# Reading already transposed tokens from DRAM in place of transposing them on TensorE, in a gated cross-attention block

## The chip, the cores and the metric

The kernel runs on one core of one Trainium2 chip. The metric is the device time of one execution in microseconds (us). Each kernel is timed in several runs and the median is given; one further execution is recorded by the hardware profiler, and every duration below is from that one.

TensorE is called PE in the profile (PEld is its weight load), VectorE DVE, ScalarE ACT, GpSimd POOL and SyncE SP. DMAs are issued from SP's queue, but for a few at the start that ACT issues.

## What is computed

The input is x, two sequences of 2048 tokens of 512 numbers (4096 tokens in all), and a context of two times 77 tokens.

```python
def layernorm(x):  # no learned scale
    return (x - mean(x)) / sqrt(var(x) + 1e-5)

x = x + tanh(g_xattn) * xattn(layernorm(x), ctx, ctx)   # 16 heads of 32, softmax over 77 keys
x = x + tanh(g_ffn) * ffn(layernorm(x))                 # 512 -> 2048 -> gelu -> 512

def qlinear(x, w, b):          # both linears of ffn
    xq, sx = quant(x)          # round(x / scale), scale = max|x| / 127 over the whole tensor
    wq, sw = quant(w)
    return (xq @ wq.T + b) * (sw * sx)
```

All arrays are float32. The maximum in the quantization is over a whole tensor, so the first linear of the feed-forward can't start before the attention of every token is done.

## The kernel before

The tokens are worked in eight blocks of 512 (`NB` = 8, `TB` = 512), numbered 0 to 7 here; each block is four tiles of 128 tokens (`NT` = 4). There are three stages: attention over blocks 0 to 7, then the first linear with gelu, then the second linear. Blocks 0 to 3 belong to the first sequence, 4 to 7 to the second.

Attention of block i goes through eight steps s = 0 to 7 (loop at lines 473 to 532). A step treats one group of four heads (g = s // 2) and half of the block's tokens (two tiles):

- `apply_v` (line 343), in even steps: softmax weights times values, for the group before. Result `pc` in PSUM, copied to `cT` by ACT.
- `softmax` (line 294), two steps ahead of the step that uses it: PE computes the scores `ps`; DVE takes the maximum (line 312) and subtracts it (316), ACT takes the exponential (322), DVE sums (324) and takes the reciprocal (326), POOL multiplies (327).
- `transpose_a` (line 333), twice: PE transposes the softmax weights (`pta`), ACT copies them to `aT`.
- `project_o` (line 358) in even steps, for the block before: output projection `po`; DVE adds it to X with the gate (line 369).
- `project_q` (line 281) in odd steps: query projection of four matmuls, each of which the profile records as two. At s = 1 and 3 it works on block i, at s = 5 and 7 on block i + 1.
- Only for the next block: `norm(i + 1)` at s = 1 (mean and variance of four tiles by two DVE instructions each, lines 159 and 160; then 1/sigma on POOL, line 163), and `transpose_x(i + 1, t)`, tiles 0 and 1 at the end of s = 3, tiles 2 and 3 at the start of s = 5. `transpose_x` (line 265) has DVE write (x - mean)/sigma (270), PE transpose it in four pieces (275, `ptx`) and ACT copy it to `xnT` (276), which `project_q` reads.
- At s = 7, for the block before: `norm2_stats` and `norm2_max` (lines 371 and 375): mean, variance and 1/sigma of the new X, then its normalized form `xf` (line 189) and the maximum of that, `tm` (line 384).
- In blocks 1 to 4 `weight_step` (line 406) has DVE prepare the feed-forward weights in odd steps: at i = 1 and 3 the maximum of a quarter of w1 or w2 (line 405), at i = 2 and 4 its quantization (lines 204 and 205). After the last maximum `diagonal_of` (line 166) makes a diagonal matrix (`diag_w`, line 171), and at s = 0 of the next block `scale_of` (line 174) puts a matmul on PE (`pg_w`, line 178) that waits for it.
- `add_bias` (line 278) on POOL.

The order on PE is the program's own (`manual_schedule` for PE). The orders on DVE, ACT and POOL are set when the kernel is built, by a list scheduler that follows the program with some freedom; `issue_after` forbids it to put an instruction ahead of a given one. Once built, each engine takes its instructions strictly in that order, and SP its DMAs too.

X blocks and the raw quarters of w1 and w2 share a pool of eight buffers of 1 MB (`xpool`), so a weight quarter is loaded when another tile has been used up. `load_x(i + 2)` stands after block i. PSUM results of `project_q`, `project_o`, `apply_v` and `scale_of` share two buffers (`ps_p`); those of the transposes share two others (`ps_t`), scores two more (`ps_s`).

Of the kernel before, what the change touches and what calls it, by code (L numbers as in the profile page):

```python
# [8 lines left out]
F32 = mybir.dt.float32  # L9
# [6 lines left out]
P = 128  # L16
D = 512
# [25 lines left out]
def tile_flamingo_gated_block(  # L43
    ctx: ExitStack,
    tc: tile.TileContext,
    x: bass.AP,
    ctxT: bass.AP,
    g_xattn: bass.AP,
# [37 lines left out]
    def kchunks(w):  # L86
        return w.rearrange("(kc p) n -> p kc n", p=P)
# [6 lines left out]
    wo_sb = awts.tile([P, KC, D], F32, name="wo_sb")  # L94
    ctx_sb = awts.tile([P, B, KC, NK], F32, name="ctx_sb")
    kblk = [awts.tile([P, NG, RK], F32, name=f"kb{b}") for b in range(B)]
    vblk = [awts.tile([NK, D], F32, name=f"vb{b}") for b in range(B)]
    work = actx.enter_context(tc.tile_pool(name="work", bufs=2))
    bv_sb = work.tile([NK, D], F32, tag="cT", name="bv_sb", bufs=7)
    bq_sb = const.tile([P, KC], F32, name="bq_sb")  # L100
    bk_sb = const.tile([P, KC], F32, name="bk_sb")
# [10 lines left out]
    def load_ctx(engine, b):  # L112
        engine.dma_start(ctx_sb[:, b, :, :], kchunks(ctxT[b]))

# [14 lines left out]
    for b in range(1, B):  # L129
        load_ctx(nc.sync, b)  # L130
    load_x(1)
    nc.sync.dma_start(wo_sb, kchunks(woT))
    nc.sync.dma_start(tg[:, 0:1], g_xattn.to_broadcast([P, 1]))
    nc.sync.dma_start(tg[:, 1:2], g_ffn.to_broadcast([P, 1]))
    nc.sync.dma_start(bo_sb, bo.to_broadcast([P, D]))
    nc.sync.dma_start(b1_sb, b1)

    ident = const.tile([P, P], F32, name="ident")
# [72 lines left out]
    with actx:  # L211
# [7 lines left out]
        def project_k(b, g):  # L219

            pk = ps_p.tile([P, 512], F32, tag="pp", name=f"pk{b}_{g}")
            for kc in range(KC):
                nc.tensor.matmul(  # L223
                    pk[:, :NK],
                    wk_sb[:, kc, g * P : (g + 1) * P],
                    ctx_sb[:, b, kc, :],
                    start=(kc == 0),
                    stop=(kc == KC - 1),
                )
            return pk  # L230
# [12 lines left out]
        def project_v(b):  # L243

            pv = ps_p.tile([P, 512], F32, tag="pp", name=f"pvv{b}")
            for kc in range(KC):
                nc.tensor.matmul(  # L247
                    pv[:NK, :],
                    ctx_sb[:, b, kc, :],
                    wv_sb[:, kc, :],  # L250
                    start=(kc == 0),
                    stop=(kc == KC - 1),
                )
            nc.vector.tensor_tensor(vblk[b], pv[:NK, :], bv_sb, ALU.add)

        ln, xnT, qT, aT, cT, es = {}, {}, {}, {}, {}, {}

        def norm(i):
# [4 lines left out]
            ln[i] = mv, rstd  # L263

        def transpose_x(i, t):
            mv, rstd = ln[i]
            if t == 0:
                xnT[i] = work.tile([P, KC, TB], F32, tag="xnT", name=f"xnT{i}", bufs=1)
            xn = work.tile([P, D], F32, tag="xn", name=f"xn{i}_{t}")
# [11 lines left out]
        def project_q(i, g):  # L281
            pq = ps_p.tile([P, TB], F32, tag="pp", name=f"pq{i}_{g}")
            for kc in range(KC):
                nc.tensor.matmul(  # L284
                    pq,
                    wq_sb[:, kc, g * P : (g + 1) * P],
                    xnT[i][:, kc, :],
                    start=(kc == 0),
                    stop=(kc == KC - 1),
                )  # L290
            qT[i, g] = work.tile([P, TB], F32, tag="qT", name=f"qT{i}_{g}", bufs=5)
            nc.scalar.activation(qT[i, g], pq, AF.Identity, bias=bq_sb[:, g : g + 1])  # L292
# [126 lines left out]
        def weight_step(i, s):  # L419
# [53 lines left out]
        for i in range(NB):  # L473
            for s in range(2 * NG):
# [42 lines left out]
                with tc.issue_after(last["DVE"]):  # L517
                    weight_step(i, s)
                    if i == NB - 1 and s == 5:

                        xs0 = work.tile([P, NT, D], F32, tag="aT", name="xs0", bufs=3)
                        for t in range(NT):
                            normalize2(xs0[:, t, :], 0, t)
                t = s - NT if i == 0 else s // 2
                if t >= 0 and (i == 0 or s % 2 == 0):
                    with tc.issue_after(last["POOL"]):
                        add_bias(i, t)
            if i + 2 < NB:
                load_x(i + 2)
            if i == 0:  # L530
# [15 lines left out]
        s_x, inv_x = scale_of(diagonal_of(xmax, "x"), "x", ps_p, "pp")  # L546
        xq0 = work.tile([P, NT, D], BF16, tag="xnT", name="xq0", bufs=1)
        for t in range(NT):
# [218 lines left out]
```

## Time and profile before

| what | value |
|---|---|
| median of 3 runs | 656.1 us (653.93 to 656.38) |
| the profiled execution's own time | 654.98 us |
| its span, first to last instruction | 653.2 us |
| what lies around the span | 1.8 us |
| mean granted PE clock | 0.986 |
| busy: PE, DVE, ACT, POOL | 625.5, 520.1, 337.3, 205.1 us |
| attention stage, 57 to 411 us: PE busy | 347.1 of 354.0 us |
| attention stage: DVE, ACT, POOL busy | 293.5, 150.3, 125.4 us |
| DMA in the attention stage | 43 GB/s, 12% of the 16 engines |

The stages follow each other: attention to about 411 us, the first linear to about 530 us, the second to the end. A busy time is a union of intervals and not a sum; consecutive DVE instructions overlap by some 0.08 us in the records, so the distance from start to start is the better price of one instruction, and it is used below.

### The profile page before, as it was taken

How to read it: one execution, taken by the hardware profiler on the slowest of the kernel's cores; microseconds unless marked ns; L12 is line 12 of the kernel's file. 1: busy time of each engine (PE TensorE's matmuls, PEld its weight loads, DVE VectorE, ACT ScalarE, POOL GpSimd, SP SyncE). 2: the span in 40 equal slices, each digit the busy share in tenths (PEclk: the TensorE clock that was granted, in tenths of full speed). 3: DMA queues.
4: the chain of work that ended last, by engine and by line, in shares of the span. 5: the costliest groups of instructions: out<-in, count | busy, mean ns of one | idle time of the engine just before them, and what ended most of it. 6: DMA issues, size and time to landing. Idle time of an engine off the chain costs nothing.

```text
span 653.2 us, 8220 instructions
## 1 busy us (share of the span) xinstructions
PE 625.5 (96%) x3048; PEld 318.2 (49%) x3048; DVE 520.1 (80%) x825; ACT 337.3 (52%) x463; POOL 205.1 (31%) x161
## 2 busy tenths in 40 slices
PE   5999999999999999999999999599999979999997
PEld 4565555555554554555555543244444434444443
DVE  5685787998998998976877768899989779877551
ACT  2365444444444354354343441298888879654530
POOL 2144333234243334233242331000000009997000
PEclk9999999999999999999999999599999999999999
DMA  9902000031131131100000000189999109799952
GB/s 281 374 35 99 31 1 1 2 129 64 65 129 69 62 129 64 66 1 0 1 1 1 2 18 0 21 285 306 334 342 331 25 0 368 251 348 347 343 196 80
DMA packets 44255, 84.90 MB, mean 130 GB/s; under 512 B 18795, under 2 KB 22891, under 8 KB 38584
## 3 DMA queue, kind: packets, MB, share of 16 engines
q1 hardware_dynamic: 43112, 83.70, 36.5%
q10 hardware_dynamic: 1104, 0.69, 0.3%
q8 instruction: 24, 0.39, 0.3%
q14 instruction: 15, 0.12, 0.1%
HBM read 49.25 MB, written 31.46 MB: 124 GB/s over the span
## 4 chain that ended last, share of the span: by engine, by line
PE 80%; DVE 15%; ACT 2%; POOL 1%; issue 1%; DMA 1%; ACTq 0%; DVEq 0%
PE pf L684 17%; PE ph L620 17%; PE po L362 14%; PE pq L284 12%; PE pta L340 7%; PE ps L303 5%; PE pc L349 3%; DVE xf L189 2%; DVE tm L384 2%; PE ptx L275 2%; DVE e L316 2%; DVE mx L312 2%; PE pvv L247 1%; DVE sm L324 1%; PE pk L223 1%; ACT e L322 1%
## 5 line engine op out<-in xcount | busy, mean ns | idle before, releaser
L327 POOL TENSOR_TENSOR e<-e,rs 128x616 f32<-128x616 f32 x64 | 78.7, 1229 | 223.1 <-DVE rs L326 148.9
L284 PE MATMUL pq<-xnT,wq_sb 128*128 128x512 f32 x256 | 115.3, 593 | 0.0
L684 PE MATMUL pf<-w2q,hq 128*128 128x512 bf16 x512 | 112.4, 383 | 2.6 <-DVE hq L205 2.0
L362 PE MATMUL po<-wo_sb,cT 128*128 128x512 f32 x256 | 114.8, 593 | 0.0
L620 PE MATMUL ph<-xqT,w1q 128*128 128x512 bf16 x512 | 113.1, 385 | 0.7 <-DVE xqT L560 0.7
L627 ACT ACTIVATE G<-ph,b1s,s 128x512 f32<-128x512 f32 x128 | 99.5, 777 | 15.1 <-PE ph L620 4.3
L341 ACT COPY aT<-pta 77x512 f32<-77x512 f32 x128 | 68.0, 581 | 68.9 <-PE pta L340 68.8
L322 ACT ACTIVATE e<-e 128x616 f32<-128x616 f32 x64 | 45.9, 717 | 87.9 <-DVE e L316 86.3
L637 DVE TENSOR_REDUCE hmax<-G 128x1 f32<-128x1024 f32 (+1 forms) x65 | 76.8, 1198 | 8.0 <-ACT G L627 7.9
L684 PEld LDWEIGHTS <-hq 128*128 128x128 bf16 x512 | 50.4, 99 | 64.3 <-issue 2.4
L620 PEld LDWEIGHTS <-w1q 128*128 128x128 bf16 x512 | 50.6, 99 | 62.9 <-issue 3.2
L340 PE MATMUL pta<-ident,e 128*77 128x128 f32 x512 | 70.2, 280 | 0.4 <-ACT xnT L276 0.4
L324 DVE TENSOR_REDUCE sm<-e 128x8 f32<-128x616 f32 x64 | 50.6, 790 | 24.4 <-ACT e L322 24.1
L362 PEld LDWEIGHTS po<-wo_sb,cT 128*128 128x128 f32 x256 | 46.4, 190 | 48.2 <-issue 46.6
L284 PEld LDWEIGHTS pq<-xnT,wq_sb 128*128 128x128 f32 x256 | 46.1, 190 | 46.1 <-issue 46.1
L677 ACT ACTIVATE Gb<-Gb,inv_h 128x2048 f32<-128x2048 f32 x22 | 43.7, 1999 | 35.7 <-DMA Gb<-h 35.7
L312 DVE TENSOR_REDUCE mx<-ps 128x8 f32<-128x616 f32 x64 | 50.2, 784 | 14.8 <-PE ps L303 14.3
L340 PEld LDWEIGHTS pta<-ident,e 128*77 128x77 f32 x512 | 55.6, 147 | 11.8 <-issue 10.3
L698 POOL TENSOR_TENSOR x<-x,b_sb 128x512 f32<-128x512 f32 x32 | 57.2, 1829 | 0.1
L303 PEld LDWEIGHTS ps<-kb,qT 64*128 64x128 f32 x512 | 36.0, 186 | 43.5 <-ACT qT L292 20.6
L316 DVE TENSOR_TENSOR e<-ps,mx 128x616 f32<-128x616 f32 x64 | 50.9, 796 | 2.5
L303 PE MATMUL ps<-kb,qT 64*128 64x154 f32 x512 | 50.6, 317 | 0.3 <-ACT qT L292 0.2
(89 smaller groups left out, 592.7 us busy)
## 6 DMA issues: line engine op xcount, KB each, us to landing
h<-G SPq DMA_DIRECT2D x22, 1024.0 KB, 5.6
Gb<-h SPq DMA_DIRECT2D x22, 1024.0 KB, 7.7
raw_w<-in_w2T SPq DMA_DIRECT2D x8, 1024.0 KB, 5.0
out_y<-x SPq DMA_DIRECT2D x32, 256.0 KB, 3.1
x<-in_x SPq DMA_DIRECT2D x7, 1024.0 KB, 5.2
raw_w<-in_w1T SPq DMA_DIRECT2D x4, 1024.0 KB, 11.7
wk_sb<-in_wkT SPq DMA_DIRECT2D x4, 256.0 KB, 5.4
wq_sb<-in_wqT SPq DMA_DIRECT2D x4, 256.0 KB, 6.3
```

The source lines that it names most:

```text
L284: nc.tensor.matmul(pq, wq_sb[:, kc, g * P : (g + 1) * P], xnT[i][:, kc, :], start=(kc == 0), stop=(kc == KC - 1),)
L303: nc.tensor.matmul(ps[:, q, u * RK : (u + 1) * RK], qT[i, g][r, t * P : (t + 1) * P], kblk[i // NBB][r, g, :], start=True, stop=True,)
L312: nc.vector.tensor_reduce(mx, sc, AX.X, ALU.max)
L316: last["DVE"] = nc.vector.tensor_tensor(e.rearrange("p u (q r k) -> p q u r k", q=NR, r=RT), sc, mx[:, :, :, :, None].to_broadcast([P, NR, ...
L327: last["POOL"] = nc.gpsimd.tensor_tensor(e4, e4, rs[:, :, :, None].to_broadcast([P, 2, HG, NK]), ALU.mult).ins
L340: nc.tensor.transpose(pt[:NK, j, :], es[i, s][:, u, j, :], ident)
L341: nc.scalar.copy(aT[i, g][:, :, t * P : (t + 1) * P], pt[:NK, :, :])
L362: nc.tensor.matmul(po, cT[i, g][:, t * P : (t + 1) * P], wo_sb[:, g, :], start=(g == 0), stop=(g == NG - 1),)
L620: nc.tensor.matmul(ph, w1q[:, kc, fc * P : (fc + 1) * P], cur[:, kc, :], start=(kc == 0), stop=(kc == KC - 1),)
L627: nc.scalar.activation(G[:, 2 * v + u, :], ph, AF.Gelu, bias=b1s[:, fc : fc + 1], scale=s1,)
L637: nc.vector.tensor_reduce(hmax[:, k + u : k + u + 1], G[:, 2 * v + u : 2 * v + u + n, :], AX.XY, ALU.max, apply_absolute_value=True,)
L684: nc.tensor.matmul(po[t], hq[:, fc, t * P : (t + 1) * P], w2q[:, fc, :], start=(fc == 0), stop=(fc == FC - 1),)
```

## The change

Blocks 2 to 7 ("3 to 8" when counted from one) no longer go through `transpose_x`. The host hands the kernel a second copy of x, `xT`, that is transposed (512 rows of 4096 tokens). `load_xT(i)` brings one block of it, 1 MB, into a buffer `xT_sb[i]` of the shape of `xnT`. POOL multiplies it in place, in four instructions of 128x512 (`scale_x`), by a row of 1/sigma that is the same in all partitions. That row is made by `spread_rstd`: one DMA writes the 512 values of 1/sigma (128 partitions by 4) into a DRAM row of 2 KB, a second reads it back into all 128 partitions.

The mean is no longer subtracted from these tokens. Instead the query weights are centred once, at s = 3 of block 1 (`center_wq`): POOL sums the four pieces of wq in three additions, PE multiplies by ones to sum over partitions, and DVE subtracts a 512th of the sum from the four pieces in place. A product with centred weights doesn't depend on a token's mean.

`norm(i + 2)` now runs in step 6 of block i, after the softmax of that step, together with `spread_rstd(i + 2)`; before, `norm(i + 1)` ran in step 1 of block i. `load_x(i + 2)` moves from behind block i to its step 2 (step 4 in block 0), and `load_xT(i + 2)` is in step 4. `scale_x(i + 1, kc)` stands in steps 1 to 4 behind the POOL instruction of the step's softmax. Block 1 keeps its transposes, tiles 2 and 3 now at the end of step 4.

Smaller edits: `xnT` has two buffers in place of one, `qT` four in place of five; the context moves from its own tile into the buffers of `cT`; the reload of two quarters of w2 in block 4 comes one odd step later.

The core of the diff (left out: a signature, the input list, the move of the context tiles):

```diff
@@ -92,11 +93,11 @@
     awts = actx.enter_context(tc.tile_pool(name="awts", bufs=1))
     wq_sb = awts.tile([P, KC, D], F32, name="wq_sb")
     wo_sb = awts.tile([P, KC, D], F32, name="wo_sb")
-    ctx_sb = awts.tile([P, B, KC, NK], F32, name="ctx_sb")
     kblk = [awts.tile([P, NG, RK], F32, name=f"kb{b}") for b in range(B)]
     vblk = [awts.tile([NK, D], F32, name=f"vb{b}") for b in range(B)]
     work = actx.enter_context(tc.tile_pool(name="work", bufs=2))
     bv_sb = work.tile([NK, D], F32, tag="cT", name="bv_sb", bufs=7)
+    ctx_sb = [work.tile([P, KC, NK], F32, tag="cT", name=f"ctx{b}", bufs=7) for b in range(B)]
     bq_sb = const.tile([P, KC], F32, name="bq_sb")
     bk_sb = const.tile([P, KC], F32, name="bk_sb")
     tg = const.tile([P, 2], F32, name="tg")
@@ -110,7 +111,7 @@
         engine.dma_start(dst[:, :, c], kchunks(src)[:, :, c])
 
     def load_ctx(engine, b):
-        engine.dma_start(ctx_sb[:, b, :, :], kchunks(ctxT[b]))
+        engine.dma_start(ctx_sb[b], kchunks(ctxT[b]))
 
     load_x(0, pieces=NT, engines=(nc.sync, nc.scalar))
     load_ctx(nc.scalar, 0)
@@ -129,11 +130,18 @@
     for b in range(1, B):
         load_ctx(nc.sync, b)
     load_x(1)
+    xT_sb = {}
+
+    def load_xT(i):
+        xT_sb[i] = work.tile([P, KC, TB], F32, tag="xnT", name=f"xT{i}", bufs=2)
+        nc.sync.dma_start(xT_sb[i], kchunks(xT[:, i * TB : (i + 1) * TB]))
+
     nc.sync.dma_start(wo_sb, kchunks(woT))
     nc.sync.dma_start(tg[:, 0:1], g_xattn.to_broadcast([P, 1]))
     nc.sync.dma_start(tg[:, 1:2], g_ffn.to_broadcast([P, 1]))
     nc.sync.dma_start(bo_sb, bo.to_broadcast([P, D]))
     nc.sync.dma_start(b1_sb, b1)
+    rows = ctx.enter_context(tc.tile_pool(name="rows", bufs=2, space=bass.MemoryType.DRAM))
 
     ident = const.tile([P, P], F32, name="ident")
     make_identity(nc, ident)
@@ -246,13 +254,14 @@
             for kc in range(KC):
                 nc.tensor.matmul(
                     pv[:NK, :],
-                    ctx_sb[:, b, kc, :],
+                    ctx_sb[b][:, kc, :],
                     wv_sb[:, kc, :],
                     start=(kc == 0),
                     stop=(kc == KC - 1),
                 )
             nc.vector.tensor_tensor(vblk[b], pv[:NK, :], bv_sb, ALU.add)
 
+        rstd_row = {}
         ln, xnT, qT, aT, cT, es = {}, {}, {}, {}, {}, {}
 
         def norm(i):
@@ -262,10 +271,36 @@
             layernorm_stats(X[i], mv, rstd, f"a{i}")
             ln[i] = mv, rstd
 
+        def spread_rstd(i):
+
+            row = rows.tile([NT, P], F32, tag="row", name=f"row{i}")
+            nc.sync.dma_start(row.rearrange("t p -> p t"), ln[i][1])
+            rstd_row[i] = work.tile([P, TB], F32, tag="rrow", name=f"rrow{i}", bufs=1)
+            nc.sync.dma_start(
+                rstd_row[i], row.rearrange("(o t) p -> o (t p)", o=1).to_broadcast([P, TB])
+            )
+
+        def scale_x(i, kc):
+
+            xs = xT_sb[i][:, kc, :]
+            nc.gpsimd.tensor_tensor(xs, xs, rstd_row[i], ALU.mult)
+
+        def center_wq():
+
+            total = work.tile([P, D], F32, tag="xn", name="wq_total")
+            nc.gpsimd.tensor_tensor(total, wq_sb[:, 0, :], wq_sb[:, 1, :], ALU.add)
+            for kc in range(2, KC):
+                nc.gpsimd.tensor_tensor(total, total, wq_sb[:, kc, :], ALU.add)
+            pm = ps_p.tile([P, D], F32, tag="pp", name="pm")
+            nc.tensor.matmul(pm, ones, total, start=True, stop=True)
+            for kc in range(KC):
+                w = wq_sb[:, kc, :]
+                nc.vector.scalar_tensor_tensor(w, pm, -1.0 / D, w, ALU.mult, ALU.add)
+
         def transpose_x(i, t):
             mv, rstd = ln[i]
             if t == 0:
-                xnT[i] = work.tile([P, KC, TB], F32, tag="xnT", name=f"xnT{i}", bufs=1)
+                xnT[i] = work.tile([P, KC, TB], F32, tag="xnT", name=f"xnT{i}", bufs=2)
             xn = work.tile([P, D], F32, tag="xn", name=f"xn{i}_{t}")
             nc.vector.tensor_scalar(
                 xn, X[i][:, t, :], mv[:, t, 0:1], rstd[:, t : t + 1], ALU.subtract, ALU.mult
@@ -284,11 +319,11 @@
                 nc.tensor.matmul(
                     pq,
                     wq_sb[:, kc, g * P : (g + 1) * P],
-                    xnT[i][:, kc, :],
+                    (xnT if i < 2 else xT_sb)[i][:, kc, :],
                     start=(kc == 0),
                     stop=(kc == KC - 1),
                 )
-            qT[i, g] = work.tile([P, TB], F32, tag="qT", name=f"qT{i}_{g}", bufs=5)
+            qT[i, g] = work.tile([P, TB], F32, tag="qT", name=f"qT{i}_{g}", bufs=4)
             nc.scalar.activation(qT[i, g], pq, AF.Identity, bias=bq_sb[:, g : g + 1])
 
         def softmax(i, s):
@@ -436,8 +471,8 @@
                 wdiag[name] = diagonal_of(wmax[name], name)
             if i == 4 and odd:
                 quantize(w2q[:, j * KC : (j + 1) * KC, :], wraw["w2", j], inv_w["w2"])
-                if j < 2:
-                    load_w("w2", w2_piece, [j + 2])
+                if j in (1, 2):
+                    load_w("w2", w2_piece, [j + 1])
 
         ordered = {mybir.EngineType.DVE, mybir.EngineType.PE, mybir.EngineType.Activation}
         with tc.manual_schedule(engines=ordered):
@@ -477,9 +512,6 @@
                     apply_v(i, g - 1)
                 elif not odd and i > 0:
                     apply_v(i - 1, NG - 1)
-                if s == 5 and i + 1 < NB:
-                    for t in (2, 3):
-                        transpose_x(i + 1, t)
                 if s + 2 < 2 * NG:
                     last = softmax(i, s + 2)
                 elif i + 1 < NB:
@@ -499,13 +531,22 @@
                     project_q(i, g + 2)
                 elif odd and i + 1 < NB:
                     project_q(i + 1, g - 2)
-                if i + 1 < NB:
+                if i == 0:
                     if s == 1:
                         with tc.issue_after(last["DVE"]):
-                            norm(i + 1)
-                    if s == 3:
-                        for t in (0, 1):
-                            transpose_x(i + 1, t)
+                            norm(1)
+                    if s in (3, 4):
+                        for t in (2 * s - 6, 2 * s - 5):
+                            transpose_x(1, t)
+                elif i + 1 < NB and 1 <= s < 1 + KC:
+                    with tc.issue_after(last["POOL"]):
+                        scale_x(i + 1, s - 1)
+                if s == 6 and i + 2 < NB:
+                    with tc.issue_after(last["DVE"]):
+                        norm(i + 2)
+                    spread_rstd(i + 2)
+                if i == 1 and s == 3:
+                    center_wq()
                 if i == 0 and 3 <= s < 7:
                     for b in range(1, B):
                         place_k(b, s - 3, project_k(b, s - 3))
@@ -521,12 +562,15 @@
                         xs0 = work.tile([P, NT, D], F32, tag="aT", name="xs0", bufs=3)
                         for t in range(NT):
                             normalize2(xs0[:, t, :], 0, t)
+                if i + 2 < NB:
+                    if s == (4 if i == 0 else 2):
+                        load_x(i + 2)
+                    if s == 4:
+                        load_xT(i + 2)
                 t = s - NT if i == 0 else s // 2
                 if t >= 0 and (i == 0 or s % 2 == 0):
                     with tc.issue_after(last["POOL"]):
                         add_bias(i, t)
-            if i + 2 < NB:
-                load_x(i + 2)
             if i == 0:
                 load_w("w1", w1_piece, range(4))
             if i == 2:
```

More of the change, by code (lines that the diff above doesn't have):

```diff
@@ L46, in tile_flamingo_gated_block @@
     x: bass.AP,
+    xT: bass.AP,
     ctxT: bass.AP,
@@ L248, in project_v @@
                     pv[:NK, :],
-                    ctx_sb[:, b, kc, :],
+                    ctx_sb[b][:, kc, :],
                     wv_sb[:, kc, :],
@@ L546, in tile_flamingo_gated_block @@
         s_x, inv_x = scale_of(diagonal_of(xmax, "x"), "x", ps_p, "pp")
-        xq0 = work.tile([P, NT, D], BF16, tag="xnT", name="xq0", bufs=1)
+        xq0 = work.tile([P, NT, D], BF16, tag="xnT", name="xq0", bufs=2)
         for t in range(NT):
@@ L737 @@
         "x": x.reshape(-1, D),
+        "xT": x.reshape(-1, D).T,
         "ctxT": np.asarray(ctx_1024).transpose(0, 2, 1),
```

## The prediction

> **What bounds the kernel now.** I read the wait table of PE first, in the attention stage. All that PE waits for there is this (engine and line, releaser, us in total, times, longest):
>
> ```profile
> PE pg_w L178 <- DVE diag_w L171: 1.5, 2, 0.8
> PE pc L349 <- ACT aT L341: 1.4, 2, 0.7
> PE ps L303 <- ACT qT L292: 0.2, 1, 0.2
> ```
>
> So PE is the bound from 57 to 411 us, nearly without a gap. The timeline of PE gives prices from start to start; here in block 3, where tiles are transposed:
>
> ```profile
> 185.82 1.04 PE L275 MATMUL ptx<-ident,xn 128*128 128x128 f32 x8
> 186.79 1.06 PE L349 MATMUL pc<-aT,vb 77*32 77x512 f32 x8
> 192.88 1.04 PE L275 MATMUL ptx<-ident,xn 128*128 128x128 f32 x8
> 193.84 0.80 PE L303 MATMUL ps<-kb,qT 64*128 64x154 f32 x8
> ```
>
> The chain of waits lists each such eight at 0.87 us. Two steps without them take 11.37 us (151.68 to 163.05), with them 12.24 (186.79 to 199.03). The groups give the rest that concerns us:
>
> ```profile
> L279 POOL TENSOR_TENSOR x<-x,bo_sb 128x512 f32<-128x512 f32 x32 | 40.6, 1268 | 0.0
> L276 ACT COPY xnT<-ptx 128x512 f32<-128x512 f32 x32 | 17.3, 587 | 13.6 <-PE ptx L275 13.4
> L270 DVE TENSOR_SCALAR xn<-x,mv,rstd 128x512 f32<-128x512 f32 x32 | 20.4, 661 | 3.5 <-POOL rstd L163 3.5
> L159 DVE BATCH_NORM_STATS2 st_a<-x 128x6 f32<-128x512 f32 x32 | 20.3, 671 | 3.1 <-DMA x<-in_x 3.1
> ```
>
> PE is full, but in the chain of waits DVE stands at every block's end: it is nearly late there. Two places show how nearly. End of block 1 (DVE, then PE): the diagonal comes last, and PE already waits for it 0.75 us.
>
> ```profile
> 109.52 0.75 DVE L369 SCALAR_TENSOR_TENSOR x<-po,tg,x 128x512 f32<-128x512 f32 x1 [0.94 <-PE po L362]
> 112.59 2.28 DVE L405 TENSOR_REDUCE max_w<-raw_w 128x1 f32<-128x2048 f32 x1
> 121.19 0.27 DVE L171 TENSOR_SCALAR diag_w<-ident,m_w 128x128 f32<-128x128 f32 x1
> 121.61 0.46 PE L178 MATMUL pg_w<-diag_w,ones 128*128 128x128 f32 x2 [0.75 <-DVE diag_w L171]
> ```
>
> End of block 2 (DVE, POOL, PE): the reciprocal at 173.18 lets POOL finish the softmax weights at 174.76, and PE transposes them at 176.26. The slack is 1.5 us.
>
> ```profile
> 161.04 1.28 DVE L204 TENSOR_SCALAR raw_w<-raw_w,inv_w 128x2048 f32<-128x2048 f32 x1
> 161.21 1.98 POOL L163 TENSOR_TENSOR rstd<-ve_f,mhalf 128x4 f32<-128x4 f32 x1 [1.56 <-DVE ve_f L162]
> 173.18 0.19 DVE L326 RECIPROCAL rs<-sm 128x8 f32<-128x8 f32 x1
> 173.54 1.22 POOL L327 TENSOR_TENSOR e<-e,rs 128x616 f32<-128x616 f32 x1 [8.28 <-DVE rs L326]
> 176.26 1.10 PE L340 MATMUL pta<-ident,e 128*77 128x128 f32 x8
> ```
>
> **What the Trainium skill says.** "SBUF — State Buffer", section "SBUF: two separate sides": DVE in a two-port mode and GpSimd take one port pair as an exclusive lock for a whole instruction. The trace agrees: 1/sigma on POOL takes 1.98 us under the quantization above and about 1.01 (its median) elsewhere. "GPSIMD Engine Reference", section "Instruction dispatch": about 2.5 cycles per element for two inputs, at 1.2 GHz 1.07 us for 512; measured 1.268, which I use. "DMA: Bandwidth & Descriptors", section "Specifications": DMAs of under 512 B are read-modify-write; the row has elements of 4 B, and no run shows one.
>
> **The change part by part.** I take the order of the changed kernel as built on each engine, and the prices above.
>
> *Transposes.* Six blocks lose two eights each on PE, on the path: 6 x 2 x 0.87 = -10.4 us. With them go 24 DVE instructions (0.46 to 0.76 us each from start to start) and 24 ACT copies (587 ns). Both engines wait for PE in those steps, so that is worth nothing there.
>
> *Centring.* The matmul with ones is two records of 0.43 us (a query projection is 3.44 us for eight): +0.86 on PE. The four DVE updates read PSUM like line 369, 0.66 us apart, 2.6 us plus a delay; PE next needs that PSUM buffer after `pc`, `ps` and `pta`, 2.7 us later: +0.15. The three POOL additions (3.8 us) are built ahead of the multiply of block 0, step 6; they can begin when PE has read tile 2 of block 1 (about 47.4) and end about 51.2, the multiply then at 52.4, needed at 56.9. Hidden; were the start 4 us later, it would cost. Sum +1.0.
>
> *Block 1's tiles 2 and 3 earlier.* The only wait beside it (0.37 us at 49.86, on their copy) goes: -0.3, with 0.1 for DVE's statistics that now stand ahead of a copy of keys in step 6.
>
> *Scaling.* 24 x 1.27 = 30 us on POOL, four per block, behind the multiply of steps 1 to 4. In two steps POOL then has two multiplies, two scalings and a bias, 2.4 + 2.5 + 1.3 = 6.2 of 11.4 us. A multiply delayed by 1.3 us has 4 to 5 us of slack in these steps. The query projection needs the last piece in step 5; I count 1.5 to 2 us of slack. Cost zero, with that cover.
>
> *The row.* 1/sigma is ready about 10 us after step 6 begins (below), POOL wants the row at about 23 to 30 us. Two DMAs: small ones took 5.2 to 7.9 us in the loaded first microseconds, the 256 KB broadcast of b2 3.0; I take 8 + 3 = 11 us, between 6 and 16. It fits; beyond some 20 us PE would stand. On SP they pass behind weight and X loads that wait for DVE steps which come earlier anyway. The six xT loads (5.2 us for 1 MB) meet 43 GB/s of traffic and have a block's time. The later reload in block 4 lands about when step 5 wants it (a DVE wait of 0 to 1 us, where DVE has 5). `qT` with four buffers suffices: the oldest is read two steps before.
>
> *Statistics in step 6.* This is the one that I cost highest. `norm(i + 2)` is 2 x 1.19 us for four `bn_stats`, some 0.35 for aggregates: 2.7 us, moved from step 1, where DVE had room, to just ahead of the crowd of step 7. The built order also bunches the four statistics of `norm2` in step 7, where three of them used to be done in earlier steps: +2.05 us. Earlier waits of DVE absorb part (0.78 for the exponential, 0.94 for `po`). I add up DVE's instructions in built order from the first maximum of step 6 (1.84 us after PE begins that step):
> - Ends of blocks 1 and 3: `diag_w` starts at 20.96 us in place of 17.96. PE waits for it: +3.0 each, +6.0.
> - Ends of blocks 2 and 4: the quantization now begins under POOL's multiply and waits for its lock (0.9 us), and one more subtraction is built ahead of the reciprocal, which starts at 25.2 in place of 21.5. POOL is done at 26.8, PE 0.1 later; it wanted 24.6: +2.3 each, +4.6.
> - End of block 5: no weights; reciprocal about 23.4, PE waits +0.5. Blocks 0, 6 and 7 have one of the two norms only: 0.
>
> *Sum.* -10.4 + 1.0 - 0.3 + 6.0 + 4.6 + 0.5 = +1.4 us. Against the profiled execution (654.98, of it 653.2 span and 1.8 around it, unchanged) that is 656.4. The median of the runs shown, 656.1, is 1.1 higher, so the forecast is 657.5.
>
> **The rivals.**
> - *The crowd costs PE nothing.* PE's slack would be larger than I add up. For: DVE is behind in four of eight blocks only, and PE shows almost no wait today. Against: it already waits for the diagonal. Time: 656.1 - 10.4 + 1.0 - 0.3 = 646.4. With half the waits (5.5 of 11.1 us) it is 652, the fastest that I hold fairly likely.
> - *The port lock deepens the crowd (slower).* Place: step 7 and the next step 0, where DVE has two quantizations and four normalizations in two-port form. If one POOL instruction (1.22 to 1.27 us: a multiply or a bias) falls on a normalization, DVE loses up to that; the timeline shows two of them taking 1.60 us beside a multiply in place of 0.9. I assumed POOL idle there. Price: 5 block ends x 1.25 = 6.2 us: 663.7. It decides from 0.4 us per end on, which puts the total 3.3 us over the time before.
> - *The row comes late.* POOL would stand at the first scaling with the softmax behind it. Each us beyond 20 costs up to six: at 22 us, +12, 669. Against: no DMA of the page takes as long.
>
> That the transposes do not go away is excluded: they are gone from the built order for six blocks.
>
> **How the numbers follow.** A measurement of this kernel can tell about 0.5%, 3.3 us, from no change. Forecast, within 3.3 us of 656.1: 0.45. First rival, with its half-way form beyond that bound: 0.22. Port lock: 0.28. Late row: 0.05. So faster 0.22, same 0.45, slower 0.33. The range reaches to the half-way case less a microsecond, 650.5, and to the port-lock case, 663.5. The forecast's own range is 653 to 659.5.
>
> **What would show it.** In the profile after: no `ptx` beyond block 1; two PE steps at 11.37 us in mid-block; a wait `pg_w <- diag_w` of some 7.5 us in two times in place of 1.5; a new wait of `pta` on POOL or DVE at the starts of blocks 3 and 5; POOL busy some 34 us more. If `pg_w` waits under 3 us in all, the crowd was over-counted and the first rival holds. If POOL waits for a DMA, it is the row. If PE waits in mid-block for `pq`, the scaling is late, which I excluded.

## The result and the profile after

| | before | after |
|---|---|---|
| median | 655.47 us (653.93 to 657.3, 6 runs) | 660.9 us (660.0 to 662.78, 6 runs) |
| profiled execution | 654.98 us, span 653.2 | 661.28 us, span 659.5 |
| mean granted TensorE clock | 0.986 | 0.981 |
| TensorE waits for `pg_w` | 1.5 us in 2 | 7.2 us in 2 |

The ratio after to before is 1.0086, with a 95% interval of 1.0062 to 1.011: the kernel became slower by just under one per cent. The forecast was 657.5 us with a range of 650.5 to 663.5. The time lies in the range, but 3.4 us above the forecast, outside the forecast's own range of 653 to 659.5, and beyond the half per cent that the forecast counted as no change.

The wait table of PE of the kernel after, in the attention stage (engine and line, releaser, us in total, times, longest):

```profile
PE pg_w L186 <- DVE xmax L423: 7.2, 2, 3.6
...
PE pta L375 <- POOL e L362: 3.4, 2, 1.7
PE pc L384 <- ACT aT L376: 1.4, 2, 0.7
PE ps L338 <- ACT qT L327: 1.4, 2, 1.2
PE pc L384 <- ACT e L357: 0.5, 2, 0.3
```

The wait for `pg_w` went from 1.5 to 7.2 us. The wait of `pta` on GpSimd (3.4) and one of 1.2 us for `qT` are new. The table names `xmax`, which ended at about 125.2 by the timeline, but what the matmul reads is the diagonal.

The timeline of PE of the kernel after, in block 3 (start, us, engine, line, operation, count; the last line is cut off by the end of the stretch):

```profile
191.52 1.06 PE L384 MATMUL pc<-aT,vb 77*32 77x512 f32 x8
192.52 0.79 PE L338 MATMUL ps<-kb,qT 64*128 64x154 f32 x8
193.24 1.10 PE L375 MATMUL pta<-ident,e 128*77 128x128 f32 x8
194.18 3.60 PE L397 MATMUL po<-wo_sb,cT 128*128 128x512 f32 x8
197.71 0.79 PE L338 MATMUL ps<-kb,qT 64*128 64x154 f32 x8
198.43 1.10 PE L375 MATMUL pta<-ident,e 128*77 128x128 f32 x8
199.37 3.60 PE L319 MATMUL pq<-xT,wq_sb 128*128 128x512 f32 x8
202.90 0.64 PE L384 MATMUL pc<-aT,vb 77*32 77x512 f32 x4
```

Two steps take 11.38 us (191.52 to 202.90), nothing is between them, and no `ptx` is left. So the transposes did come off the path. They were given back at the ends of blocks. The timeline of DVE at the end of block 1, for the kernel after:

```profile
107.57 1.28 DVE L167 BATCH_NORM_STATS2 st_a<-x 128x6 f32<-128x512 f32 x2
...
113.80 1.25 DVE L167 BATCH_NORM_STATS2 st_f<-x 128x6 f32<-128x512 f32 x2
...
116.46 2.27 DVE L440 TENSOR_REDUCE max_w<-raw_w 128x1 f32<-128x2048 f32 x1
...
124.90 0.28 DVE L179 TENSOR_SCALAR diag_w<-ident,m_w 128x128 f32<-128x128 f32 x1
```

and that of PE at the same place:

```profile
125.33 0.46 PE L186 MATMUL pg_w<-diag_w,ones 128*128 128x128 f32 x2 [3.59 <-DVE xmax L423]
125.72 1.30 PE L338 MATMUL ps<-kb,qT 64*128 64x154 f32 x8
126.94 1.99 PE L375 MATMUL pta<-ident,e 128*77 128x128 f32 x8
```

Read the second pair of numbers, too. Behind the wait, `ps` takes 1.30 us in place of 0.79 and `pta` 1.99 in place of 1.10, though nothing is waited for there. The reason is in the table of stretches of the kernel after (stretch, its length, then busy time and count of PE, PEld, DVE, ACT and POOL, then the granted PE clock, the DMA share and GB/s):

```profile
121.00:125.00 4.00, 0.74 (x2) 0.00 (x0) 4.00 (x9) 0.51 (x1) 0.00 (x0) 1.00 0.07 9
125.00:129.00 4.00, 3.67 (x19) 3.27 (x20) 3.78 (x11) 0.61 (x2) 2.12 (x2) 0.61 0.30 61
129.00:133.00 4.00, 4.00 (x15) 1.36 (x15) 3.35 (x4) 1.53 (x3) 0.80 (x2) 0.97 0.00 0
```

TensorE is idle for 3.6 us, and in the next 4 us its clock is 0.61 in the mean: 0.50 from 125.87 to 129.28, and 1.00 before and behind. In those stretches DVE is busy without a gap up to the diagonal: the stall is of its making.

The end of block 2 shows the other form, POOL and then PE, for the kernel after:

```profile
170.55 1.91 POOL L171 TENSOR_TENSOR rstd<-ve_f,mhalf 128x4 f32<-128x4 f32 x1 [2.01 <-DVE ve_f L170]
180.60 1.22 POOL L362 TENSOR_TENSOR e<-e,rs 128x616 f32<-128x616 f32 x1 [8.14 <-DVE rs L361]
```

```profile
181.87 1.10 PE L375 MATMUL pta<-ident,e 128*77 128x128 f32 x8 [1.73 <-POOL e L362]
```

GpSimd stands 8.14 us for a reciprocal of DVE. It stood as long before the change (8.28 us), but then the softmax weights were ready 1.5 us before TensorE wanted them; now they come too late, and TensorE waits 1.73 us. The last line pair, of the groups after, is that of the work put on GpSimd and of the centring:

```profile
L286 POOL TENSOR_TENSOR xT<-xT,rrow 128x512 f32<-128x512 f32 x24 | 30.4, 1268 | 0.0
L298 DVE SCALAR_TENSOR_TENSOR wq_sb<-pm,wq_sb 128x512 f32<-128x512 f32 x4 | 2.5, 684 | 0.5 <-PE pm L295 0.5
```

The multiplies take 1268 ns each as assumed, with no idle time ahead of them: GpSimd never waited for the row.

### The profile page after: what moved, and what is told of

Same layout as the page of the kernel before. It is cut to its first block, busy times and chain, and to the rows that moved or that the text cites. A ratio compares the mean times of both kernels' runs of the same rounds, so it can differ in the third digit from the quotient of the medians.

```text
span 659.5 us, 8041 instructions
## 1 busy us (share of the span) xinstructions
PE 620.7 (94%) x2954; PEld 311.1 (47%) x2954; DVE 508.3 (77%) x805; ACT 325.8 (49%) x439; POOL 235.7 (36%) x188
## 4 chain that ended last, share of the span: by engine, by line
PE 73%; DVE 22%; POOL 2%; ACT 1%; issue 1%; DMA 1%; DVEq 0%; POOLq 0%; ACTq 0%
PE pf L728 17%; PE ph L664 17%; PE po L397 11%; PE pq L319 11%; PE pta L375 6%; PE ps L338 5%; PE pc L384 3%; DVE e L351 3%; DVE mx L347 3%; DVE st_a L167 2%; DVE tm L419 2%; DVE xf L197 2%; DVE sm L359 2%; DVE st_f L167 2%; PE pk L231 1%; POOL rstd L171 1%
## 5 line engine op out<-in xcount | busy, mean ns | idle before, releaser
L319 PE MATMUL pq<-xT,wq_sb 128*128 128x512 f32 x192 | 87.1, 596 | 0.0
L375 PE MATMUL pta<-ident,e 128*77 128x128 f32 x512 | 72.0, 285 | 3.4 <-POOL e L362 3.4
L375 PEld LDWEIGHTS pta<-ident,e 128*77 128x77 f32 x512 | 57.1, 150 | 15.2 <-issue 9.2
L319 PEld LDWEIGHTS pq<-xT,wq_sb 128*128 128x128 f32 x192 | 35.1, 193 | 34.9 <-issue 34.6
```

Of the source, the lines that this page charges most:

```text
L319: nc.tensor.matmul(pq, wq_sb[:, kc, g * P : (g + 1) * P], (xnT if i < 2 else xT_sb)[i][:, kc, :], start=(kc == 0), stop=(kc == KC - 1),)
L375: nc.tensor.transpose(pt[:NK, j, :], es[i, s][:, u, j, :], ident)
```

## The experiments

The theory: the transposes are worth their full time on TensorE, and it goes back because the statistics in step 6 join VectorE's crowd at the ends of blocks; TensorE waits there, and then runs at a low clock for some microseconds. Rivals: the multiplies on GpSimd or the row cost it; or TensorE would wait for VectorE in any case once it is faster.

**The statistics alone.** The kernel before, which keeps its transposes; only loads and statistics are a block ahead (the lines that move the loads, as in the change, are not shown).

```diff
+                if s == 6 and i + 2 < NB:
+                    with tc.issue_after(last["DVE"]):
+                        norm(i + 2)
...
-                    if s == 1:
+                    if i == 0 and s == 1:
                         with tc.issue_after(last["DVE"]):
-                            norm(i + 1)
+                            norm(1)
```

> The kernel before, with only the loads and the statistics of x moved a block ahead (statistics in step 6); transposes on TensorE, subtraction of the mean and query weights stay as before, nothing is scaled on GpSimd. Theory (the crowd on VectorE at the block ends costs the time): the waits of TensorE seen in the changed kernel appear here too, some 7 us for the diagonal in two times, 2 us at the starts of blocks 3 and 5, 1.2 us at block 6, and slow matmuls after the long waits, so about 13 us over before: 668 to 670. Rival (scaling on GpSimd, its port lock or the row cost the time): no change, 655 to 657.

Measured: 671.92 us (670.9 to 672.67), ratio 1.0251 (1.0236 to 1.0267), 16.6 us more than before. Its wait table of PE is nearly that of the kernel after:

```profile
PE pg_w L178 <- DVE xmax L388: 7.2, 2, 3.6
PE pta L340 <- POOL e L327: 4.0, 3, 1.8
```

So neither scaling, nor row, nor centring is needed for the loss, and it isn't that TensorE became too fast. (That the loads have moved too isn't the cause: they stand as early in the runs below that lose nothing.) The moved statistics bring others with them. In the 18 us ahead of the first `pg_w`, VectorE has eight `bn_stats` in this run and in the kernel after, four of them those of `norm2`, where the kernel before has one. Some 2 us above the expectation are low clock: it is 0.50 from 123.47 us for 6.83 us, and from 229.28 and from 287.31 for 3.41 us each, and the matmuls there take 6.0 us longer in all, where 3.2 were expected. From here to the kernel after (660.9) the rest of the change gives 11.0 us.

**The rest alone.** The kernel after with statistics back in step 1 of the block ahead, where the kernel before has them. In a first form the row and the multiplies stayed, the multiplies in steps 3 and 4, two in each (the lines that move these two are not shown).

```diff
-                if s == 6 and i + 2 < NB:
+                if s == 1 and 1 <= i and i + 1 < NB:
                     with tc.issue_after(last["DVE"]):
-                        norm(i + 2)
-                    spread_rstd(i + 2)
+                        norm(i + 1)
```

> The kernel after with the statistics of a block back in step 1 of the block ahead of it, where the kernel before has them, the row's two transfers after them, and the four multiplies by the row in steps 3 and 4, two in each. Tokens still come transposed, and query weights are centred. Theory (the loss is where the statistics stand, at the crowded end of the blocks; the transposes are worth 10.4 us on TensorE, less 0.9 for centring): the pg_w waits fall to 0.75 each, no slow clock behind them, no waits at blocks 3 and 5, and 655.5 - 10.4 + 0.9 = 644 to 648 us. Rival (taking the transposes out makes TensorE so early that it waits for VectorE at the ends of blocks wherever the statistics stand): 653 to 660 us.

Measured: 681.79 us (680.22 to 683.83), ratio 1.0403 (1.0368 to 1.0438). Both theories missed, since the edit brought a new stall. POOL and then PE in block 3 of this run:

```profile
207.09 2.49 POOL L286 TENSOR_TENSOR xT<-xT,rrow 128x512 f32<-128x512 f32 x2 [7.84 <-DMA rrow<-row]
```

```profile
208.41 5.97 PE L319 MATMUL pq<-xT,wq_sb 128*128 128x512 f32 x8 [5.17 <-POOL xT L286]
```

The row came too late for the multiplies, and the projections waited for them, 22.9 us in all. This is the rival "the row comes late" of the prediction, forced. Within the wait of 5.17 us the clock fell to 0.50, and the eight matmuls behind it took 5.97 us in place of 3.60. But it isn't the clock that made them slow. Ahead of block 7, at full clock and behind a wait of only 0.74 us, the eight take as long from first to last, in two halves, since the second half needs the other two multiplies:

```profile
361.89 2.35 PE L319 MATMUL pq<-xT,wq_sb 128*128 128x512 f32 x4 [0.74 <-POOL xT L286]
365.51 2.35 PE L319 MATMUL pq<-xT,wq_sb 128*128 128x512 f32 x4 [1.27 <-POOL xT L286]
```

At the ends of blocks 1 and 3 `pg_w` waited 0.75 us each, as before the change, and the waits at blocks 3 and 5 were absent; that part of the theory held. Instruction by instruction against the next run, all the time that TensorE lost (34 us) arises at the six late projections, 20 us ahead of them and 14.5 us within them; a wait of VectorE for a w2 piece (7.2 us) adds nothing to it. To see what the transposes are worth, the row and the multiplies were left out:

```diff
-                elif i + 1 < NB and s in (3, 4):
-                    with tc.issue_after(last["POOL"]):
-                        scale_x(i + 1, 2 * s - 6)
-                        scale_x(i + 1, 2 * s - 5)
...
-                        spread_rstd(i + 1)
```

> The statistics of a block back in step 1 of the block ahead of it, without the row and without the multiplies by it (blocks 2 to 7 are left unscaled by 1/sigma, so their attention is computed on other numbers). In the run with the row the multiplies came too late for the projections (TensorE waited 22.9 us for them), which hid what it was to show. Theory (the transposes taken from TensorE are worth their 10.4 us when VectorE's crowd at the ends of blocks is as before; the centring costs 0.9): pg_w waits of 0.75 us each, none at blocks 3 and 5, and 655.4 - 10.4 + 0.9 = 644 to 648 us. Rival (with the transposes gone TensorE waits for VectorE wherever the statistics stand): 653 to 660 us.

Measured: 645.82 us (644.58 to 647.2), ratio 0.9851 (0.9827 to 0.9875), 9.4 us under before. Its waits of PE:

```profile
PE pg_w L186 <- DVE diag_w L179: 1.5, 2, 0.8
PE pc L384 <- ACT aT L376: 1.4, 2, 0.7
...
PE ps L338 <- ACT qT L327: 0.2, 1, 0.2
```

These are the three lines of the kernel before, with the same numbers. The transposes are worth what was counted, 10.4 less 0.9, when the statistics stand in step 1. The rival, that TensorE waits wherever they stand, is refuted.

**No scaling.** The kernel after without the multiplies and the row.

```diff
-                elif i + 1 < NB and 1 <= s < 1 + KC:
-                    with tc.issue_after(last["POOL"]):
-                        scale_x(i + 1, s - 1)
...
-                    spread_rstd(i + 2)
```

> The kernel after without the scaling of the transposed tokens: no multiplies by the row on GpSimd and no transfers of the row (blocks 2 to 7 are left unscaled by 1/sigma, so their attention is computed on other numbers). Theory (the 24 multiplies of 1.27 us and the row lie beside other work and cost nothing; the loss is VectorE's crowd of statistics): 659 to 662 us, with waits at pg_w of 3.6 us twice and at blocks 3 and 5 of 1.7 us. Rival (the multiplies' hold on the memory port slows VectorE's quantizations and copies, and that is part of the crowd): 650 to 656 us.

Measured: 661.6 us (660.37 to 662.53), ratio 1.0084 (1.006 to 1.0108), with the same waits of 3.6, 3.6, 1.7 and 1.7 us. Thirty microseconds of GpSimd and twelve transfers cost nothing that can be measured here.

**Keeping TensorE busy.** The kernel after with four needless matmuls in the gap ahead of `pg_w`.

```diff
+        if name in ("w1", "w2"):
+            for kc in range(KC):
+                nc.tensor.matmul(pg, ones, wo_sb[:, kc, :], start=True, stop=True)
         nc.tensor.matmul(pg[:, :P], ones, diag, start=True, stop=True)
```

> The changed kernel with four needless matmuls of 128x512 in front of the matmul that waits for the diagonal, so that TensorE works through most of the 3.6 us; their result is overwritten. Theory (an idle TensorE gets a lower clock for some us afterwards): the wait falls to about 0.2 us each, the matmuls behind it run at their usual 0.8, 1.1 and 3.6 us, and 3.2 us are gained: 657 to 658. Rival (the slow matmuls behind the wait have another cause, such as late operands): they stay slow, 660.5 to 661.5.

Measured: 658.65 us (658.26 to 661.14), ratio 1.0061 (1.0037 to 1.0085): more work, and 2.2 us less time than the kernel after. The stretches of this run, the same as above:

```profile
121.00:125.00 4.00, 3.93 (x17) 1.79 (x16) 4.00 (x10) 0.00 (x0) 0.00 (x0) 1.00 0.15 23
125.00:129.00 4.00, 4.00 (x21) 2.31 (x18) 3.97 (x8) 1.78 (x3) 2.44 (x2) 1.00 0.21 43
```

The clock stays at 1.00. So the idle time itself lowered it, and the low clock had a price of its own. The intervals of the two ratios overlap (1.0037 to 1.0085, and 1.0062 to 1.011), so it is the two profiles that settle the amount: the matmuls behind the two gaps take 3.2 us less, as expected. In this execution 1.7 us are lost again at block 5, where the clock is 0.50 from 276.85 for 3.41 us behind a wait of 1.73, and 1.2 us are gained at the start, where TensorE reached its full clock earlier.

**The matmul of the weight scale a step later.**

```diff
-            if i in (2, 4) and s == 0:
+            if i in (2, 4) and s == 1:
```

> The changed kernel with the matmul that waits for the diagonal put behind step 1 of blocks 2 and 4 in place of step 0; the statistics stay in step 6. Theory: the two waits of 3.6 us and the slow matmuls behind them (1.6 us each) go, the waits at the starts of blocks 3 and 5 stay; about 10 us under the changed kernel: 650 to 652. If the softmax weights of step 2 are late there too, as at blocks 3 and 5, some 2 us each come back: 653 to 655. Rival (the waits only move to the next late thing in full): 659 to 661.

Measured: 652.31 us (649.86 to 655.05), ratio 0.9963 (0.995 to 0.9977). The waits for `pg_w` are gone, 0.56 and 0.55 us of other waits stand in their place, and those at blocks 3, 5 and 6 remain. The medians differ by 8.6 us, the profiles by 9.6. In the profiles 9.7 us are gained at the two ends of blocks (the waits, 7.2 us less 1.1, and the low clock behind them) and 1.4 at the start, and 1.7 are lost to a low clock at block 5.

**Statistics two steps earlier.** In step 4, where VectorE has room.

```diff
-                if s == 6 and i + 2 < NB:
+                if s == (6 if i == 0 else 4) and i + 2 < NB:
```

> The changed kernel with norm and spread_rstd of block i + 2 in step 4 in place of step 6 (block 0 keeps step 6). Theory (crowd at the block ends): the waits for the diagonal fall from 7.2 to about 1.5 us, those at the starts of blocks 3 and 5 go, no slow matmuls; about 14 us under the changed kernel: 646 to 649. Rival (scaling on GpSimd or the row): as the changed kernel, 660 to 661.

Measured: 656.95 us (654.75 to 657.82), ratio 1.002 (1.001 to 1.0029). A miss by some 8 us. The waits for `pg_w` fell to 2.1 us and those at block 3 went, but at the start of block 5 TensorE stood for 2.94, 2.88 and 1.74 us. What DVE waits for in this run, and then SP's timeline, show why:

```profile
DVE raw_w L212 <- DMA raw_w<-in_w2T: 7.8, 1, 7.8
```

```profile
241.42 0.37 SPq L277 DMA_DIRECT2D row<-rstd  x1
250.48 0.34 SPq L279 DMA_DIRECT2D rrow<-row  x1
250.87 0.42 SPq L435 DMA_DIRECT2D raw_w<-in_w2T  x1
```

The second transfer of the row waits for the first, from 241.8 to 250.5, and a reload of a w2 piece is queued behind it on SP. VectorE reaches the quantization of that piece and waits 7.8 us, with the softmax behind it. The first attempt to move the transfers back, on top of that edit:

```diff
+                if s == 6 and i + 2 < NB:
                     spread_rstd(i + 2)
```

> The kernel after with the statistics of block i+2 in step 4 of block i (step 6 in block 0, as before), but the two transfers of the row still issued in step 6. The run with both in step 4 took 656.95 us: the waits at pg_w fell, but in block 4 the second transfer of the row stood on SP for 9 us ahead of a reload of a w2 piece, VectorE waited 7.84 us for that piece, and TensorE then stood about 7.6 us behind it. Theory (that wait is the queue's order on SP, nothing of the statistics): with the transfers back in step 6 the wait of VectorE for raw_w is gone, and the time is 656.95 - 7.6 - about 1.5 of slow clock = 647 to 650 us. Rival (the statistics in step 4 make VectorE late for the quantization in step 5 by themselves): 655 to 658 us, with the same waits of pta and pc around the start of block 5.

Measured: 657.35 us (655.26 to 657.93), ratio 1.0021 (1.0012 to 1.003), DVE's wait 7.7 us. It tested nothing: SP's order isn't written out by hand, and the scheduler put the two transfers ahead of the reload again. The same holds for the run with both moves:

> The kernel after with statistics in step 4, the row's transfers in step 6, and the matmul pg_w of the weight scale in step 1 of blocks 2 and 4 in place of step 0. Theory (moving pg_w saved the two waits and the slow clock behind them, 660.9 to 652.3 us; the statistics' place holds the waits at blocks 3 and 5, 3.9 us, and at block 6, 1.2 us): 652.3 - 5.1 = 645 to 648 us. Rival (the two moves mend the same two ends of blocks and nothing more): 651 to 653 us.

Measured: 656.58 us (656.25 to 663.48), ratio 1.0026 (1.0005 to 1.0048), DVE's wait for the reload 8.1 us. TensorE's wait for the scale also came back in another form, as `pc` waiting 1.92 and 1.32 us on VectorE's reading of `pg_w`. For the order to change, the data had to come later. In block 4 the last two instructions of the statistics now wait for step 6 (the lines that split them off are not shown):

```diff
+                if s == (6 if i == 0 else 4) and i + 2 < NB:
+                    with tc.issue_after(last["DVE"]):
+                        norm(i + 2, i == 4)
+                    if i != 4:
+                        spread_rstd(i + 2)
+                if i == 4 and s == 6:
                     with tc.issue_after(last["DVE"]):
-                        norm(i + 2)
+                        rest.pop()()
                     spread_rstd(i + 2)
```

> Statistics in step 4 once more, but in block 4 the last two instructions of them (variance plus epsilon, and the power on GpSimd) wait for step 6, so that in the order of SP the row's two transfers really stand behind the reload of the w2 piece. (In the run e1b_trip_step6 the scheduler put them ahead of it again, so that run did not test its edit.) Theory (VectorE's wait of 7.7 us for raw_w in block 4 came from the transfer of the row that stood for 9 us ahead of the reload on SP, and TensorE's stall at the start of block 5 from that wait): no wait of VectorE for raw_w, no waits of pta and pc at block 5, and 656.95 - 7.6 - about 1.5 of slow clock = 646 to 650 us. Rival (VectorE is late there for its own work, statistics ahead of the quantization in step 5): 654 to 658 us with the same waits at block 5.

Measured: 646.65 us (646.25 to 647.52), ratio 0.9865 (0.9845 to 0.9886). SP's timeline in this run, where the reloads come first, and its wait table of PE:

```profile
232.56 11.87 SPq L444 DMA_DIRECT2D raw_w<-in_w2T  x2
248.16 0.37 SPq L286 DMA_DIRECT2D row<-rstd  x1
257.22 0.34 SPq L288 DMA_DIRECT2D rrow<-row  x1
```

```profile
PE pg_w L195 <- DVE diag_w L188: 2.1, 2, 1.4
PE pc L393 <- ACT aT L385: 1.4, 2, 0.7
...
PE ps L347 <- ACT qT L336: 0.4, 2, 0.2
```

VectorE waits for no piece any more, and TensorE's waits are within 1 us of those before the change. This is the whole computation with everything the change wanted, 14.2 us under the kernel after and 8.5 under that before: four `bn_stats` per block stand two steps earlier, those of `norm2` are spread out again (three `bn_stats` in the 18 us ahead of the first `pg_w`, in place of eight), and one transfer doesn't block another.

Last, a mixture: `pg_w` in step 1, and statistics in step 4 only in the three blocks whose ends still stalled.

```diff
-            if i in (2, 4) and s == 0:
+            if i in (2, 4) and s == 1:
...
-                if s == (6 if i == 0 else 4) and i + 2 < NB:
+                if s == (6 if i in (0, 1, 3) else 4) and i + 2 < NB:
```

> pg_w in step 1 of blocks 2 and 4, and the statistics in step 4 only in blocks 2, 4 and 5 (in blocks 0, 1 and 3 they stay in step 6; in block 4 the last two instructions and the row's transfers stay in step 6 too). Theory (with pg_w in step 1, 652.3 us are left with waits of 2.0 us at block 3, 2.0 at block 5 and 1.2 in block 6, all from statistics in step 6 of blocks 2, 4 and 5): 652.3 - 5.2 = 646 to 649 us, with none of these three waits. Rival (with these waits gone TensorE runs into the next late step of VectorE within the same block, as in the run with both moves): 651 to 656 us.

Measured: 647.21 us (646.65 to 647.71), ratio 0.9869 (0.9845 to 0.9893). The waits at blocks 3 and 5 fell from 2.0 to 0.9 us. It is no better than the run before it: at the ends of blocks 1 and 3, where the statistics still stand in step 6, a later `pg_w` serves as well as earlier statistics.

## Why the prediction was right in kind and 3.4 us short

Term by term, the prediction against the two profiled executions (timeline of PE at the same instructions, rounded):

| term | predicted, us | seen, us |
|---|---|---|
| transposes | -10.4 | -10.4 |
| centring | +1.0 | +0.9 |
| block 1's tiles earlier | -0.3 | +0.35 (the wait is 0.52 in place of 0.37) |
| scaling, row | 0 | 0 |
| ends of blocks 1 and 3, waits | +6.0 | +5.7 |
| the same, low clock behind them | not in the sum | +3.2 |
| ends of blocks 2 and 4 | +4.6 | +4.0 |
| end of block 5 | +0.5 | +1.2 |
| start | not in the sum | +1.4 |
| sum | +1.4 | +6.3 |

That the time fell inside the wide range is in part luck: the upper end, 663.5, was put there for a rival that wasn't at work, and the range made no room for a slow clock.

- *Transposes and centring*: right, and not only by the timeline: the run with statistics in step 1 gained 9.4 us for -10.4 + 0.9.
- *Block 1's tiles earlier*: wrong in sign, by 0.65 us. The wait didn't go with the move; one for a copy of ScalarE came in its place, 0.15 us longer, and the other 0.2 us lie in the matmuls around it.
- *Scaling and row at zero*: right. Removing both changed nothing. The 1.07 us for a multiply in the prediction is an estimate only; 1268 ns was measured, before and after. The row was estimated at 11 us between 6 and 16; SP's second transfer waited 8.5 us in the mean for the first (50.8 us in six), and the broadcast took 4.9 to landing, some 13 us together.
- *Statistics in step 6*: right in place and nearly in size. Counting VectorE's instructions in their built order gave the diagonal 20.96 us after TensorE begins the step; it came 20.8 us after (104.11 to 124.90). For the reciprocal it was 25.2 against 25.0 (155.28 to 180.24). The lock of GpSimd, put at 0.9 us there, shows as a quantization of 1.99 us (at 167.62) in place of 1.28. The new waits at blocks 3 and 5 are there as predicted.
- *What failed* is the price of those waits. The step "PE waits for it: +3.0 each" charged an idle TensorE with the idle time and nothing else. Behind each of the two, `ps`, `pta` and `pq` took about 1.6 us longer in all, while the clock was 0.50 for 3.41 us. These 3.2 us are the largest term that the sum lacked, and the filler run, which closes the gaps, took them back. The Trainium skill has the rule that should have been in the sum: "TensorE: Matmul & The Clock Gate", section "Part 1: The HAM clock gate (the "warmup" mystery)", says that the clock falls to half after at least one idle window of about 3.4 us. A wait forecast at 3 us over the 0.75 already there, 3.75 us, is longer than that. The traces agree in that the clock fell to 0.50 behind 3.6 us and behind 5.17 us (the run with the late row), but an interval idle throughout isn't needed: it fell behind 1.72 us too, as the last section shows, and there the measurement decides.
- *The end of block 5* was priced at 0.5 us for a wait of `pta`; it came as a wait of `ps` for `qT` of 1.2 us, on ScalarE's queue, behind an exponential that waited for VectorE.
- *The start*, 1.4 us, is of work that the change doesn't touch, or hardly. The first projection of queries began at 15.92 us in this execution and at 14.86 before, and took 4.00 us in place of 3.67. In ten of the eleven experiments' profiles it began at 14.38 to 15.46 and took 3.64 to 3.69; in one (no scaling) it was 15.68 and 3.99. The records of the clock show why: the full clock begins at 16.64 us in this execution and at 16.37 in the one without scaling, but at 13.81 in the kernel before and at 12.34 to 15.02 in the other ten. The same section says that the ramp at the start varies from run to run. That fits; no run ties these 1.4 us to the change.
- *The rivals*: "the crowd costs PE nothing" is refuted by the kernel with statistics alone. "The port lock deepens the crowd" ended near the right time (663.7) for a wrong reason: normalizations took 1.00 us for two, as without a lock. "The row comes late" wasn't so in the change, but is what happened once statistics and scaling were in the same block.

## What to carry to other kernels

Taking work from a full engine gains its time only if the helper beside it isn't made later by the same edit: count the helper's instructions, in built order, up to the one that the full engine waits for. A stall of TensorE can cost more than its length: charge one of 3.4 us or more with some 1.6 us of slow matmuls behind it as well, and treat one from 1.7 us on as a risk of the same. Move work to a step in which the helper waits anyway. With a transfer that waits for another one, look at what is queued behind it on the issuing engine, and in whose hands that order lies.

## What the runs showed of the hardware

- TensorE's clock after idle time. In the clock records of all 13 profiled executions it is 1.00 or 0.50 and nothing between; 0.61 above is a mean. Within one execution it changes only at points that are whole multiples of 3.413 us apart (the worst is off by 0.001 us). Between these points lie intervals of equal length. Three of them in the kernel after, the first behind the wait of 3.59 us and the other two around the wait of 1.72 us at block 5 (columns as in the table of stretches above):

```profile
125.87:129.28 3.41, 3.41 (x17) 2.88 (x18) 3.19 (x9) 0.89 (x2) 2.40 (x2) 0.50 0.10 26
276.06:279.47 3.41, 2.62 (x18) 0.75 (x16) 3.17 (x7) 1.55 (x3) 0.07 (x1) 1.00 0.91 306
279.47:282.88 3.41, 2.21 (x11) 1.51 (x12) 2.33 (x4) 2.45 (x5) 3.41 (x3) 1.00 0.11 39
```

And two of the run with `pg_w` in step 1, around the same wait:

```profile
266.23:269.64 3.41, 1.69 (x17) 0.62 (x13) 2.67 (x6) 1.59 (x3) 1.28 (x2) 1.00 0.85 310
269.64:273.05 3.41, 3.41 (x10) 2.44 (x11) 1.79 (x5) 1.78 (x3) 3.41 (x3) 0.50 0.01 4
```

In the kernel after, the wait is shared by two intervals; TensorE works for 2.62 and 2.21 us of 3.41, and the clock stays. In the other run it lies in one, TensorE works for 1.69 us, and the clock falls in the next. By the traces, from 25 us on, each of the 43 falls in the 13 executions follows an interval in which TensorE was idle for at least 0.505 of it; of the 2298 intervals at full clock that no fall follows, three were idle for more than half (0.505, 0.551 and 0.579). So what decides is not the length of a wait but whether it leaves one interval idle for half. Waits of 1.7 to 2.9 us went both ways; all 23 of 3.4 us and more brought a fall. What sets where the intervals lie isn't shown; it differs between the executions.

- A transfer of 2 KB with elements of 4 bytes from SBUF to DRAM held back its reader for 8.5 us in the mean and 9.9 at most, longer than the w2 pieces of 1 MB take to land (7.1 us in the median of the run with statistics in step 4). The Trainium skill ("DMA: Bandwidth & Descriptors", section "Specifications") has transfers of under 512 B as read-modify-write; the time is from these runs, and none of them shows that this is its cause.
